# Running products of decays: the scan kept in program order, its second operand made by ScalarE in place, its rows in a buffer of their own

## The chip, the cores and the metric

The kernel runs on one core of one Trainium2 chip. The metric is device time in microseconds of that core. It has five engines with queues of their own: PE (TensorE, matmul), DVE (VectorE), ACT (ScalarE), POOL (GpSimd) and SP (SyncE, which here only issues DMAs). The kernel before takes 4147.79 us, the median of 3 runs (4133.58 to 4149.68).

## The reference, cut to what matters

A block takes x of 2 batches, 2048 tokens and 512 features and returns x + attention(xn) + experts(xn), with xn the layer norm of x. The attention is a gated delta rule over 16 heads of 128:

```python
q = silu(conv(x @ Wq)); k = silu(conv(x @ Wk)) * DK ** -0.5; v = silu(conv(x @ Wv))
alpha = sigmoid(x @ Wa + ba); beta = sigmoid(x @ Wb + bb)
def step(S, inps):                      # over 2048 tokens
    qt, kt, vt, at, bt = inps
    err = einsum('bhvk,bhk->bhv', S, kt) - vt
    S = at * S - bt * (err outer kt)
    return S, einsum('bhvk,bhk->bhv', S, qt)
```

and then a norm of each head, a gate and the product with Wo. The experts are 16, of which each of 512 tokens uses 4.

## The kernel before, in words

Tokens are taken in chunks of 128 (C), four chunks to a block of 512 (BLK), four blocks to a batch. Heads go in pairs (HG = 2). A pair of heads over one batch is a unit u; there are 16 units, 8 to a batch. Inside a chunk the token-by-token recurrence is replaced by matrix products, which need for each chunk a 128x128 matrix of decays: entry (j, i) is beta of token j times the product of alpha over the tokens j + 1 to i.

`keys(u)` (L163 to L221) makes what does not depend on the state. For each of four blocks and two heads it projects the keys (`proj`, L146), runs the convolution and silu (`conv_silu`, L124: on ACT a copy `raw` and a scaled copy `cv` out of PSUM, on DVE three taps, L137, on ACT the silu), and after a `yield` multiplies the keys with themselves (L201, bank `pk` of PSUM), makes the decay matrices of four chunks and multiplies both into `aT` (L214).

The four decay matrices come out of one running product. A row of 516 values (four times a zero and 128 alphas) is loaded to all 128 partitions (`row`, L180 to L184: a DMA from `a_d` of 258 KB into a tile `decA`, two buffers). POOL multiplies the matrix `unit` (a zero column and a unit matrix), repeated four times, with the betas of each chunk into `start` (L208, one buffer). DVE's `tensor_tensor_scan` (L212) computes state = row * state + start along the row, in place on the row: at each chunk the zero resets it, the diagonal puts beta in, and the alphas multiply on. The result is stored to `dec_d` (L213), read by `aT` (L214), and the next row is asked for (L218). `aT` is stored (L220).

`inverses(u)` (L223) inverts 32x32 blocks on POOL by some 60 small products in turn. `projection(n)` makes q, v and the gate of one block. `before`, `after` and `output` (L512, L580, L647) are the parts of a chunk step: matrix inverse from its blocks, state, output with its norm. In `after` the variance goes DVE (L641), POOL to the power of -1/2 (L642), and in `output` back to DVE (L656, `o`).

`recurrence(b, first)` (L668) walks the chunk steps of a batch in six ticks each and takes a step of every generator in turn; `keys(u + 2)` gets a step at ticks 0 and 3, so that its 16 steps fill the first 8 of a unit's 16 chunks. Units 0 and 1 have their keys made in the opening (`firsts`, L472), with the inverses of unit 0 between them. Batch 0 has the experts woven in (L894); `out_chunk` (L766) multiplies with Wo.

This nest is the program order. A planner then orders each engine's queue: it takes instructions by priority as soon as its own estimate has their operands ready, and so moves some ahead of their place in the program. Each engine runs its queue in the order written.

Of the kernel before, what the change touches and what calls it, by code (L numbers as in the profile page):

```python
# [7 lines left out]
F32 = mybir.dt.float32  # L8
I32 = mybir.dt.int32
AF = mybir.ActivationFunctionType  # L10
ALU = mybir.AluOpType
# [3 lines left out]
P = 128  # L15
NB, T, HID = 2, 2048, 512
H, D, KS = 16, 128, 4
C = 128
# [3 lines left out]
CB = BLK // C  # L22
NKT = HID // P
HG = 2
# [9 lines left out]
DW = C + 1  # L34
# [8 lines left out]
def block_kernel(ctx, tc, x, wq, wk, wv, wg, wo, wa, wb, ba, bb, par, consts,  # L43
                 topk_idx, topk_w, ew0, ew1, ew2, ewd0, ewd1, out):
    nc = tc.nc
# [7 lines left out]
    def bank(pool, tag):  # L53
        return pool.tile([P, 512], F32, tag=tag, name=tag)


    unit = cp.tile([P, DW], F32)
# [24 lines left out]
    for i in range(1, NQ, 2):  # L82
# [6 lines left out]
    bt = {}  # L89
# [8 lines left out]
            for p in range(3)]  # L98
# [4 lines left out]
    a_d = [dp.tile([H, NC * DW], F32, name=f"a_d{b}") for b in range(NB)]  # L103
    gin_d = [dp.tile([H, T], F32, name=f"gin_d{b}") for b in range(NB)]
    dec_d = [[[dp.tile([P, CB * HG * DW], F32, name=f"dec_d{b}_{p}_{k}") for k in range(NBK)]
              for p in range(NP)] for b in range(NB)]
# [13 lines left out]
    ap = ctx.enter_context(tc.tile_pool(name="first", bufs=1))  # L120
# [3 lines left out]
    def conv_silu(ps, p, h0, h, blk, dst):  # L124

        raw = cvp.tile([P, KS - 1 + BLK], F32, tag="raw", name="raw")
        if blk == 0:
            nc.gpsimd.memset(raw[:, 0:KS - 1], 0.0)
        else:
            nc.gpsimd.tensor_copy(raw[:, 0:KS - 1], halo[p][h])  # L130
        nc.scalar.copy(raw[:, KS - 1:], ps)  # L131
        if blk < NBK - 1:
            nc.gpsimd.tensor_copy(halo[p][h], raw[:, BLK:])  # L133
        cv = cvp.tile([P, BLK], F32, tag="cv", name="cv")
        nc.scalar.activation(cv, ps, AF.Identity, bias=cbias(p, h0 + h), scale=tap(p, h0 + h, KS - 1))  # L135
        for j in range(KS - 2, -1, -1):
            nc.vector.scalar_tensor_tensor(  # L137
                cv, raw[:, j:j + BLK], tap(p, h0 + h, j), cv, ALU.mult, ALU.add)
        nc.scalar.activation(dst, cv, AF.Silu)
# [6 lines left out]
    def proj(w, h, xt):  # L146
        ps = bank(ps_p, "p")
        for k in range(NKT):
            nc.tensor.matmul(ps, lhsT=w[:, k, h * D:(h + 1) * D], rhs=xt[k],  # L149
                             start=(k == 0), stop=(k == NKT - 1))  # L150
        return ps
# [4 lines left out]
    def beta_of():  # L156
        return ap.tile([P, NC, H], F32, tag="bt", name="bt")

    def load_wk(u):
        if u < NB * NP and u not in wks:  # L160
            wks[u] = load_w(ap, "wk", wk, u % NP * HG, f"wk{u}")

    def keys(u, xts, bank_k=(ps_p, "p")):  # L163

        b, hp = divmod(u, NP)
        h0 = hp * HG
        load_wk(u)
        w = wks[u]
        if u == NP:
            bt[b] = beta_of()
            nc.sync.dma_start(out=bt[b], in_=bt_d)
        n = CB * DW

        def row(blk, h):  # L180
            dec = ap.tile([P, n], F32, tag="decA", name="decA", bufs=2)
            nc.sync.dma_start(
                out=dec, in_=a_d[b][h0 + h, blk * n:(blk + 1) * n].partition_broadcast(P))
            return dec  # L184

        dec = row(0, 0)
        for blk in range(NBK):
            xt = xts(b, blk)
            for h in range(HG):
                ps = proj(w, h, xt)  # L190
                kt = ap.tile([P, BLK], F32, tag="kf", name="kf", bufs=2)
                conv_silu(ps, 1, h0, h, blk, kt)
                if (blk, h) == (NBK - 1, HG - 1):
                    if u + 1 != NP + 2:
                        load_wk(u + 1)
                nc.sync.dma_start(out=k_d[u][blk][h], in_=kt)
                yield
                pk = bank(*bank_k)
                for c in range(CB):
                    a = kt[:, c * C:(c + 1) * C]  # L200
                    nc.tensor.matmul(pk[:, c * C:(c + 1) * C], lhsT=a, rhs=a, start=True, stop=True)  # L201
                aT = ap.tile([P, CB, C], F32, tag="aTf", name="aTf", bufs=2)

                start = ap.tile([P, n], F32, tag="start", name="start")
                a = bt[b][:, blk * CB:(blk + 1) * CB, h0 + h:h0 + h + 1]
                nc.gpsimd.tensor_tensor(  # L208
                    start.rearrange("p (c j) -> p c j", c=CB),
                    bass.AP(unit.tensor, unit.offset, [unit.ap[0], (0, CB), unit.ap[1]]),  # L210
                    bass.AP(a.tensor, a.offset, [a.ap[0], a.ap[1], (0, DW)]), ALU.mult)
                nc.vector.tensor_tensor_scan(dec, dec, start, 0.0, ALU.mult, ALU.add)  # L212
                nc.sync.dma_start(out=dec_d[b][hp][blk][:, h * n:(h + 1) * n], in_=dec)  # L213
                nc.vector.scalar_tensor_tensor(  # L214
                    aT, pk.rearrange("p (c j) -> p c j", c=CB), -1.0 / D,
                    dec.rearrange("p (c j) -> p c j", c=CB)[:, :, 0:C], ALU.mult, ALU.mult)
                if (blk, h) != (NBK - 1, HG - 1):
                    dec = row(blk + (h + 1) // HG, (h + 1) % HG)  # L218
                o = h * NC + blk * CB
                nc.sync.dma_start(out=aT_d[u][:, o:o + CB, :], in_=aT)  # L220
                yield  # L221
# [124 lines left out]
    with ExitStack() as es:  # L346
# [125 lines left out]
        def firsts():  # L472
            for u in range(2):
                for _ in keys(u, get_xT, (ps_o, "o")):
                    yield
                if u == 0:
                    drain(inverses(0))
                    yield
# [189 lines left out]
    def recurrence(b, first):  # L668
# [21 lines left out]
        for m, at in enumerate([*steps, None, None]):  # L690
# [4 lines left out]
            if at:  # L695
                n, c = at
                u, blk = blocks[n]
                ci = blk * CB + c
                if c == 0:
                    for _ in nxt:  # L700
                        pass
                    nxt = projection(n + 1) if n + 1 < (b + 1) * NP * NBK else none
                    if blk == 0:
                        for _ in ks:
                            pass
                        if u + 2 < NB * NP:
                            ks = keys(u + 2, get_xT if (u + 2) // NP == b else ahead)
                        inv = inverses(u + 1) if u + 1 < NB * NP else None
                        if inv:
                            next(inv)  # L710
                if u == NB * NP - 1:

                    if ci == 1:
                        wos = load_wo(b)
                    if ci >= 4:
                        if c == 0:
                            slots.append(big())
                        for _ in last:
                            pass
                        last = out_chunk(b, ci - 4, wos, slots[ci % len(slots)])  # L720
# [290 lines left out]
```

## Time and profile before

| | us |
|---|---|
| median of 3 runs | 4147.79 (4133.58 to 4149.68) |
| profiled execution, its own time | 4144.64 |
| span of the profile, first to last instruction | 4142.8 |
| PE busy | 3870.6 |
| DVE busy | 2348.7 |
| POOL busy | 1909.0 |
| ACT busy | 1493.0 |
| mean granted PE clock | 0.981 of full |

The profile is one execution. A group's row gives line, engine, operation, output and inputs, shapes and count, then busy time and mean ns of one, then how long the engine stood idle just before these instructions and what released it. A busy PE is not PE at its peak, since the ends of matmuls are modelled.

### The profile page before, as it was taken

To read this page: it belongs to the slowest core of one execution; us is meant where nothing else is said; L and a number is where in the kernel's file an instruction comes from. 1 tells how busy PE (TensorE), PEld (TensorE's weight loads), DVE (VectorE), ACT (ScalarE), POOL (GpSimd) and SP (SyncE) were. 2 spreads that over 40 slices of the span, in tenths; PEclk is the share of its full clock that TensorE was granted. 3 is DMA by queue.
4 is the path that set the end of the run, shared out by engine and by line. 5 is a ranking of instruction groups with operands and counts; after the bars stand their busy time and mean duration, and the time that the engine had idled before them with its cause. 6 is when DMAs were issued, how large, how long until landed. Compare 5 with 4: busy or idle time off the path is not lost.

```text
span 4142.8 us, 58432 instructions
## 1 busy us (share of the span) xinstructions
PE 3870.6 (93%) x18046; PEld 2485.1 (60%) x18046; DVE 2348.7 (57%) x6132; ACT 1493.0 (36%) x3512; POOL 1909.0 (46%) x3624
## 2 busy tenths in 40 slices
PE   8789999999999999999989999999999999999999
PEld 6456666666666665656554456566656565666554
DVE  6655565565555557676651156666666666666221
ACT  3233333333333334444430034444444443444110
POOL 1556465474554645464550045454555555473100
PEclk9899999999999999999989999999999999999999
DMA  5455546455454544454564344343334334334322
GB/s 160 157 171 169 163 139 178 133 167 157 142 161 132 158 135 121 111 148 126 164 184 125 109 119 116 104 116 107 114 109 114 112 108 112 108 85 118 103 94 76
DMA packets 579701, 541.32 MB, mean 131 GB/s; under 512 B 354689, under 2 KB 421761, under 8 KB 574273
## 3 DMA queue, kind: packets, MB, share of 16 engines
q1 hardware_dynamic: 557280, 456.18, 37.9%
q0 software_dynamic: 22112, 81.41, 6.6%
q8 instruction: 147, 2.41, 0.2%
q14 instruction: 162, 1.32, 0.1%
HBM read 363.69 MB, written 173.67 MB: 130 GB/s over the span
## 4 chain that ended last, share of the span: by engine, by line
PE 40%; DVE 14%; DMA 8%; ACT 4%; POOL 4%; issue 3%; SPq 1%; POOLq 0%; DVEq 0%; ACTq 0%
PE p L149 16%; PE p L780 10%; DVE cv L137 8%; DMA decA<-a_d 5%; POOL qg L310 2%; PE c L605 2%; DVE decA L212 2%; PE c L614 2%; ACT cv L135 1%; PE l L535 1%; PE c L595 1%; PE p L931 1%; PE o L628 1%; PE o L631 1%; ACT raw L131 1%
## 5 line engine op out<-in xcount | busy, mean ns | idle before, releaser
L137 DVE SCALAR_TENSOR_TENSOR cv<-raw,prm,cv 128x512 f32<-128x512 f32 x1152 | 947.7, 823 | 261.8 <-ACT cv L135 245.9
L149 PE MATMUL p<-xT,wv 128*128 128x512 f32 x1024 | 488.4, 604 | 9.5 <-DVE xgT L921 5.7
L131 ACT COPY raw<-p 128x512 f32<-128x512 f32 x384 | 222.8, 580 | 745.5 <-PE p L149 722.2
L149 PE MATMUL p<-xT,wq 128*128 128x512 f32 x1024 | 482.1, 600 | 1.1 <-DVE act L934 0.6
L149 PE MATMUL p<-xT,wg 128*128 128x512 f32 x1024 | 476.6, 597 | 0.3
L780 PE MATMUL p<-wo,oTf 128*128 128x512 f32 x1024 | 454.8, 596 | 1.5 <-DMA oTf<-oT_d 1.5
L149 PE MATMUL p<-xT,wk 128*128 128x512 f32 x896 | 417.9, 604 | 1.9 <-ACT cv L135 1.2
L656 DVE TENSOR_SCALAR o<-o,mv,rs 128x128 f32<-128x128 f32 x512 | 187.1, 405 | 286.2 <-POOL rs L642 286.2
L780 PEld LDWEIGHTS p<-wo,oTf 128*128 128x128 f32 x1024 | 191.2, 192 | 220.0 <-issue 216.5
L564 POOL COPY inv<-iT 32x32 f32<-32x32 f32 x512 | 143.1, 279 | 357.4 <-DVE top L559 192.9
L208 POOL TENSOR_TENSOR start<-unit,bt 128x516 f32<-128x516 f32 x128 | 162.3, 1268 | 302.5 <-DVE decA L212 269.1
L135 ACT ACTIVATE cv<-p,prm 128x512 f32<-128x512 f32 x384 | 300.8, 783 | 0.2
L212 DVE TENSOR_TENSOR_SCAN decA<-decA,start 128x516 f32<-128x516 f32 x128 | 161.5, 1262 | 245.8 <-DMA decA<-a_d 168.2
L245 POOL TENSOR_TENSOR Y<-Y,t 128x30 f32<-128x30 f32 (+14 forms) x480 | 275.0, 573 | 36.9
L549 POOL TENSOR_TENSOR kg<-kv,gd 128x256 f32<-128x256 f32 x256 | 179.4, 701 | 235.1 <-ACT kv L547 229.4
L242 POOL TENSOR_TENSOR t<-Y 128x30 f32<-128x30 f32 (+14 forms) x480 | 269.7, 562 | 38.0 <-issue 0.2
L642 POOL TENSOR_TENSOR rs<-rs,mhalf 128x2 f32<-128x2 f32 x256 | 184.1, 719 | 206.0 <-DVE rs L641 198.1
L149 PEld LDWEIGHTS p<-xT,wv 128*128 128x128 f32 x1024 | 180.0, 194 | 154.4 <-issue 140.7
L149 PEld LDWEIGHTS p<-xT,wg 128*128 128x128 f32 x1024 | 180.6, 192 | 151.8 <-issue 151.1
L149 PEld LDWEIGHTS p<-xT,wq 128*128 128x128 f32 x1024 | 181.0, 193 | 150.2 <-issue 148.2
L133 POOL COPY halo<-raw 128x3 f32<-128x3 f32 x288 | 80.4, 279 | 400.1 <-ACT raw L131 392.9
L149 PEld LDWEIGHTS p<-xT,wk 128*128 128x128 f32 x896 | 162.9, 194 | 153.6 <-issue 151.0
(176 smaller groups left out, 7293.4 us busy)
## 6 DMA issues: line engine op xcount, KB each, us to landing
decA<-a_d SPq DMA_DIRECT2D x128, 258.0 KB
dec_d<-decA SPq DMA_DIRECT2D x128, 258.0 KB
decB<-dec_d SPq DMA_DIRECT2D x64, 516.0 KB
k_d<-kf SPq DMA_DIRECT2D x128, 256.0 KB
k<-k_d SPq DMA_DIRECT2D x64, 512.0 KB
aT_d<-aTf SPq DMA_DIRECT2D x128, 256.0 KB
gin<-gin_d SPq DMA_DIRECT2D x128, 256.0 KB
oT_d<-oT SPq DMA_DIRECT2D x256, 128.0 KB
```

The source lines that it names most:

```text
L131: nc.scalar.copy(raw[:, KS - 1:], ps)
L135: nc.scalar.activation(cv, ps, AF.Identity, bias=cbias(p, h0 + h), scale=tap(p, h0 + h, KS - 1))
L137: nc.vector.scalar_tensor_tensor(cv, raw[:, j:j + BLK], tap(p, h0 + h, j), cv, ALU.mult, ALU.add)
L149: nc.tensor.matmul(ps, lhsT=w[:, k, h * D:(h + 1) * D], rhs=xt[k], start=(k == 0), stop=(k == NKT - 1))
L208: nc.gpsimd.tensor_tensor(start.rearrange("p (c j) -> p c j", c=CB), bass.AP(unit.tensor, unit.offset, [unit.ap[0], (0, CB), unit.ap[1]]), ...
L212: nc.vector.tensor_tensor_scan(dec, dec, start, 0.0, ALU.mult, ALU.add)
L242: nc.gpsimd.tensor_tensor(t, bass.AP(col.tensor, col.offset, [col.ap[0], (Q, j), (0, n)]), bass.AP(row.tensor, row.offset, [row.ap[0], (0, ...
L245: nc.gpsimd.tensor_tensor(Y[:, 0:j, j + 1:], Y[:, 0:j, j + 1:], t, ALU.add)
L549: nc.gpsimd.tensor_tensor(kg, kv[:, 0], bcast(gd1[b][:, ci, hs], D), ALU.mult)
L642: nc.gpsimd.tensor_tensor(rs, rs, mhalf[:, 0:HG], ALU.pow)
L656: nc.vector.tensor_scalar(o[:, h, :], po[:, h * D:(h + 1) * D], mv[:, h, 0:1], rs[:, h:h + 1], ALU.subtract, ALU.mult)
L780: nc.tensor.matmul(py, lhsT=oT[:, h, :], rhs=wos[h], start=(h == 0), stop=(h == H - 1))
```

## The change

The row gets a tile `row` of its own (one buffer). The two `decA` buffers now hold the scan's second operand and its result: ACT fills each of the four chunks with `unit` scaled by the beta of each partition, and the scan works in place on that. POOL's product and its `start` tile are gone. The four activations and the scan are marked `keep_in_program_order`: such an instruction is issued behind the one that the program traced before it on its engine; what comes later in the program may still be moved ahead of it.

```diff
-        def row(blk, h):
-            dec = ap.tile([P, n], F32, tag="decA", name="decA", bufs=2)
+        def ask(blk, h):
+            row = ap.tile([P, n], F32, tag="row", name="row")
             nc.sync.dma_start(
-                out=dec, in_=a_d[b][h0 + h, blk * n:(blk + 1) * n].partition_broadcast(P))
-            return dec
+                out=row, in_=a_d[b][h0 + h, blk * n:(blk + 1) * n].partition_broadcast(P))
+            return row
...
-                start = ap.tile([P, n], F32, tag="start", name="start")
-                a = bt[b][:, blk * CB:(blk + 1) * CB, h0 + h:h0 + h + 1]
-                nc.gpsimd.tensor_tensor(
-                    start.rearrange("p (c j) -> p c j", c=CB),
-                    bass.AP(unit.tensor, unit.offset, [unit.ap[0], (0, CB), unit.ap[1]]),
-                    bass.AP(a.tensor, a.offset, [a.ap[0], a.ap[1], (0, DW)]), ALU.mult)
-                nc.vector.tensor_tensor_scan(dec, dec, start, 0.0, ALU.mult, ALU.add)
-                nc.sync.dma_start(out=dec_d[b][hp][blk][:, h * n:(h + 1) * n], in_=dec)
+                dec = ap.tile([P, CB, DW], F32, tag="decA", name="decA", bufs=2)
+                for c in range(CB):
+                    ci = blk * CB + c
+                    tc.keep_in_program_order(nc.scalar.activation(
+                        dec[:, c, :], unit, AF.Identity, scale=bt[b][:, ci, h0 + h:h0 + h + 1]))
+                flat = dec.rearrange("p c j -> p (c j)")
+                tc.keep_in_program_order(
+                    nc.vector.tensor_tensor_scan(flat, row, flat, 0.0, ALU.mult, ALU.add))
+                nc.sync.dma_start(out=dec_d[b][hp][blk][:, h * n:(h + 1) * n], in_=flat)
                 nc.vector.scalar_tensor_tensor(
-                    aT, pk.rearrange("p (c j) -> p c j", c=CB), -1.0 / D,
-                    dec.rearrange("p (c j) -> p c j", c=CB)[:, :, 0:C], ALU.mult, ALU.mult)
+                    aT, pk.rearrange("p (c j) -> p c j", c=CB), -1.0 / D, dec[:, :, 0:C],
+                    ALU.mult, ALU.mult)
                 if (blk, h) != (NBK - 1, HG - 1):
-                    dec = row(blk + (h + 1) // HG, (h + 1) % HG)
+                    row = ask(blk + (h + 1) // HG, (h + 1) % HG)
```

More of the change, by code (lines that the diff above doesn't have):

```diff
@@ L178, in keys @@
         n = CB * DW
-        def row(blk, h):
-            dec = ap.tile([P, n], F32, tag="decA", name="decA", bufs=2)
+        def ask(blk, h):
+            row = ap.tile([P, n], F32, tag="row", name="row")
             nc.sync.dma_start(
-                out=dec, in_=a_d[b][h0 + h, blk * n:(blk + 1) * n].partition_broadcast(P))
-            return dec
-        dec = row(0, 0)
+                out=row, in_=a_d[b][h0 + h, blk * n:(blk + 1) * n].partition_broadcast(P))
+            return row
+        row = ask(0, 0)
         for blk in range(NBK):
```

## The prediction

> **What bounds the kernel now.** I read the page first: busy times, the chain that ended last, the costliest groups.
>
> ```profile
> span 4142.8 us, 58432 instructions
> PE 3870.6 (93%) x18046; PEld 2485.1 (60%) x18046; DVE 2348.7 (57%) x6132; ACT 1493.0 (36%) x3512; POOL 1909.0 (46%) x3624
> PE 40%; DVE 14%; DMA 8%; ACT 4%; POOL 4%; issue 3%; SPq 1%; POOLq 0%; DVEq 0%; ACTq 0%
> PE p L149 16%; PE p L780 10%; DVE cv L137 8%; DMA decA<-a_d 5%; POOL qg L310 2%; PE c L605 2%; DVE decA L212 2%; PE c L614 2%; ACT cv L135 1%; PE l L535 1%; PE c L595 1%; PE p L931 1%; PE o L628 1%; PE o L631 1%; ACT raw L131 1%
> ...
> L656 DVE TENSOR_SCALAR o<-o,mv,rs 128x128 f32<-128x128 f32 x512 | 187.1, 405 | 286.2 <-POOL rs L642 286.2
> L208 POOL TENSOR_TENSOR start<-unit,bt 128x516 f32<-128x516 f32 x128 | 162.3, 1268 | 302.5 <-DVE decA L212 269.1
> L212 DVE TENSOR_TENSOR_SCAN decA<-decA,start 128x516 f32<-128x516 f32 x128 | 161.5, 1262 | 245.8 <-DMA decA<-a_d 168.2
> ```
>
> TensorE is busy 93% of the span and sets the end; but the chain passes for 5% of the span (207 us) through the load of the decay rows and for 2% through the scan on them. The scan's row says why: VectorE stands idle 245.8 us before its 128 scans. Next I asked for the scan's line: what it waits for, and who waits for it.
>
> ```profile
> its engine sat idle before it (us, times) until:
>   DMA decA<-a_d: 168.2, 78
>   issue: 32.4, 7
>   DMA a<-aT_d: 23.0, 6
> ...
> who waited for it (us, times):
>   POOL start L208: 269.1, 89
> ```
>
> Between 300 and 3600 us these waits are 239.5 us (158.1 before 2200, 81.4 after 2400); before 300 us they are 5.5. Then VectorE's timeline at one scan:
>
> ```profile
> 3231.14 2.33 DVE L137 SCALAR_TENSOR_TENSOR cv<-raw,prm,cv 128x512 f32<-128x512 f32 x3 [0.21 <-ACT cv L135]
> 3235.53 1.23 DVE L212 TENSOR_TENSOR_SCAN decA<-decA,start 128x516 f32<-128x516 f32 x1 [2.07 <-DMA decA<-a_d]
> 3236.68 3.35 DVE L137 SCALAR_TENSOR_TENSOR cv<-raw,prm,cv 128x512 f32<-128x512 f32 x3
> 3239.96 0.20 DVE L558 STREAM_TRANSPOSE iT<-l 128x32 f32<-128x32 f32 x1
> ```
>
> The row was asked for at 3231.06 and the scan could start 4.47 us later. The planner put the scan ahead of three conv taps and the transpose that the next inverse needs; all of them stand behind it. TensorE's next wait, 0.79 us at 3240.35, is for exactly that work (top, L559). So a late row becomes TensorE idle, in part. How much, the stretches by stage tell. The first half of each of fourteen units (8 chunks) carries eight scans, the second none:
>
> ```profile
> 491.00:638.00 147.00, 139.44 (x697) 92.69 (x695) 85.63 (x204) 53.52 (x126) 84.87 (x146) 0.99 0.51 153
> 752.00:900.00 148.00, 140.44 (x703) 94.75 (x702) 88.61 (x205) 53.69 (x126) 82.25 (x144) 0.98 0.48 144
> 1013.00:1167.00 154.00, 141.40 (x703) 93.67 (x702) 86.68 (x206) 53.94 (x127) 85.02 (x145) 0.98 0.49 145
> 1284.00:1436.00 152.00, 138.73 (x692) 92.28 (x691) 87.60 (x206) 54.13 (x128) 82.57 (x145) 0.99 0.48 146
> 2721.00:2806.00 85.00, 80.49 (x413) 53.94 (x414) 56.47 (x167) 39.99 (x100) 43.29 (x91) 1.00 0.41 115
> ```
>
> Columns: length, then busy us (instructions) of PE, PE loads, DVE, ACT, POOL, clock, DMA. The first four hold the same work. Idle before their scans was 23.0, 23.6, 34.0 and 31.6 us: 9.5 us more idle in the later pair goes with 5.5 us more length, a rate of 0.58. The last line has no scans and 4.5 us of PE idle in 85 (5.3%), the same share as scan halves of that time (2603 to 2721: 6.3 in 118). So there is structural idle too, which the change can't take.
>
> **The Trainium skill.** Perfetto Trace Analysis, Tensor Engine Instruction, says that VectorE, ScalarE and GpSimd are strict first-in first-out: one late operand holds all behind it. The timeline agrees. SBUF — State Buffer, Who interferes with whom, says that a VectorE instruction with two SBUF inputs contends with a GpSimd one that reads SBUF. Here the three taps beside a "start" product took 3.35 us in place of 3 x 0.751 (L137's median). ScalarE: Activation LUTs, What ACT_TABLE_LOAD costs, prices an ACTIVATE at 186 ns + 0.833 ns per element + 93 ns per pointer operand, with 93 ns overlap back to back; for cv (512 elements, two pointers) that gives 798 ns, and the trace has 783.
>
> **The change, part by part.** The order of TensorE's instructions hardly moves (some 250 of 9,900 stand elsewhere, many in the opening), so I cost the rest against this one.
>
> 1. Scan kept in program order: on VectorE it now stands behind L641 (rs) and ahead of o (L656), not ahead of taps. Its row is asked for right after the scan before, 14.9 us earlier in a scan half (119 us by 8), against the 4.3 to 4.5 us of the load. Removed: the 239.5 us of idle after 300 us.
> 2. Its new place is where VectorE waits for GpSimd's power (L642) anyway: in 2603 to 2721 that is 6.3 us over 8 waits, 0.79 each. Over 112 scans about 88 us of scan time falls into this wait. If GpSimd answers sooner now, less; bounds 0 to 138 (112 x 1.23).
> 3. GpSimd loses 128 x 1.268 = 162 us and the 269 us in which "start" stood at the head of its queue waiting for the scan, with inv, kg, rs and halo copies behind. VectorE also loses the contention: from 0 to (3.35 - 2.25) = 1.1 us a scan; I take 0.3, 34 us over 112.
> 4. ScalarE gains 512 activations of 128x129, one pointer. Estimate from the ScalarE page: 186 + 107 + 93 = 387 ns, four back to back 4 x 387 - 3 x 93 = 1.27 us. From this trace: copies of 512 and 256 columns (580, 381) give 281 ns for 128, and half of oT's excess over the 256 copy (563 - 381 = 182) makes 372 ns, 1.49 us without overlap. So 142 to 167 us after 300 us, and 20 to 24 before. They mostly stand behind the inv copies (L572) and ahead of or behind oT; next come q, inv (L576), raw and cv. ScalarE usually waits there: L576 and the others idle 0.3 to 2 us for PE or VectorE. I charge 5 us; without that cover it is the whole 1.27.
> 5. The row buffer is single (before, two decA buffers took the rows), and SP issues dec_d and then the next row. From scan to scan that is at least 1.23 + 0.32 + 0.4 + 4.3 = 6.3 us. In the opening the eight scans run from 86.2 to 120.75 us, 4.9 us apart; 7 x 1.3 = 9 us later, and unit 0's inverses wait behind them. Against it, GpSimd sheds some four "start" products with their waits between 125 and 200 us, where it is the busiest (18.6 of 20 us at 160 to 180): 6 to 10 us. I take 0, bounds -10 to +15.
> 6. aT and its bank of PSUM come some 1.6 us later behind the scan and one o; VectorE is ahead by the 2.07 us wait removed plus 1.23 of scan, so nothing. The DMAs are the same in number and size.
>
> **The sum.** Parts 1 to 3 free 239.5 + 88 + 34 = 361 us of VectorE. TensorE can't give all of that back: its visible idle in the fourteen halves is 2009 - 1890.9 = 118 us. At 0.58 part 1 alone would be 139 us, which exceeds it; at the unscanned share nothing would go. I take 55% of the idle: -65. With +5 (part 4) and 0 (part 5): -60. On the profiled execution's own 4144.6 us that is 4084.6; the median shown stands 3.2 higher (4147.8), so 4087.
>
> **The rivals.**
> - The pairs' rate holds in full: idle hidden behind modelled matmul ends comes back too. -139 less 5, some 4010. For it: the 207 us of chain. Against: the cap of 118 us.
> - Hidden anyway: VectorE only catches up later and PE's idle share stays at 5.3%, as in the halves without scans. Gain 0 to 20, about 4138.
> - Slower: ScalarE's blocks of four hold up oT, raw and cv, on which TensorE's PSUM banks wait. They price at 163 to 190 us; against -65 they decide from a pass-through of 0.37, and reach +0.5% at 0.5. At 0.6 of 175: +105 - 65, 4188. For it: strict order, and PE's two-deep banks. Against: ScalarE is 36% busy and waited 722 us for L149.
> - The change doesn't do what it says: GpSimd's power now comes late behind Y products, or the scan waits for its activations in place of the row. VectorE's wait would only change its name; the time is that of the second rival, and it shares its chance.
>
> **How the numbers follow.** Likeliest (-30 to -100): 0.50. Full rate: 0.22. Hidden: 0.16. Slower: 0.12. About 0.5%, 21 us, is what a measurement of this kernel can tell from no change. Faster 0.72, same 0.16, slower 0.12. The range from 4020 to 4148 leaves out the deepest part of the full rate and the slower case; the likeliest alone is 4048 to 4118.
>
> **What would show it.** Scan's idle for its row: near 0 (right), or replaced by ACT decA in step 4's place (wrong). Scan halves shorter by 3 to 5 us after 2400 and by 4 to 10 before 1500; halves without scans unchanged at 84 to 85. o's wait for rs down by some 80 us. ScalarE busy 1493 + 163 to 190. First eight scans 6.3 us apart. The prediction fails if oT, w or raw on ScalarE begin later relative to their matmuls and PE's waits for them grow.

## The result and the profile after

The changed kernel takes 4078.46 us (median of 4 runs, 4071.89 to 4085.75); the kernel before, run beside it, takes 4141.59 (4 runs, 4133.58 to 4149.68). The ratio is 0.9848, 95% interval 0.9817 to 0.9879: 63 us faster. The profiled execution took 4071.89 us, 72.8 less than that of before.

These are lines of the page of the changed kernel: span, busy times, the chain that ended last by engine and by line, and five groups. Lines of code behind L208 have moved down by one.

```profile
span 4070.1 us, 58930 instructions
PE 3825.9 (94%) x18046; PEld 2463.9 (61%) x18046; DVE 2337.3 (57%) x6132; ACT 1642.1 (40%) x4025; POOL 1822.5 (45%) x3496
PE 45%; DVE 12%; POOL 6%; ACT 5%; issue 2%; DMA 1%; SPq 0%; POOLq 0%; ACTq 0%; DVEq 0%
PE p L149 20%; PE p L781 11%; DVE cv L137 7%; POOL rs L643 2%; ACT cv L135 2%; PE c L615 2%; PE c L606 2%; POOL qg L311 2%; PE l L536 1%; PE o L629 1%; PE c L596 1%; PE o L632 1%; ACT raw L131 1%; PE p L932 1%; DVE o L657 1%
...
L149 PE MATMUL p<-xT,wk 128*128 128x512 f32 x896 | 417.2, 604 | 36.8 <-DVE aTf L215 29.7
L657 DVE TENSOR_SCALAR o<-o,mv,rs 128x128 f32<-128x128 f32 x512 | 194.8, 404 | 237.7 <-POOL rs L643 237.7
L643 POOL TENSOR_TENSOR rs<-rs,mhalf 128x2 f32<-128x2 f32 x256 | 229.0, 894 | 203.2 <-DVE rs L642 196.0
```

The row's load and the scan have left the chain: its DMA share is 1% where it was 8%. Two things are new. GpSimd's power (L643) is on it with 2%, at a mean of 894 ns where it had 719. And the key projections wait 29.7 us for `aT` (L215); before, they had 1.9 us of idle time in all. The scan's own line in the changed kernel shows what became of its wait:

```profile
L213 DVE TENSOR_TENSOR_SCAN decA<-row,decA x128: 1216/1225/2330, 86.7 to 3469.9; 128x516 f32<-128x516 f32 x128
...
its engine sat idle before it (us, times) until:
  DMA row<-a_d: 9.2, 9
who waited for it (us, times):
```

168.2 us of waiting for the row is 9.2, and nobody waits for the scan any more. The activations that make the operand (their line in the changed kernel) cost what the estimate said, a median of 390 ns against 387:

```profile
L209 ACT ACTIVATE decA<-unit,bt x512: 360/390/416, 77.1 to 3466.9; 128x129 f32<-128x129 f32 x171
```

The stretches of the changed kernel that answer to those of before, from the same chunk step to the same chunk step (columns as before: length; busy us and count of PE, PE loads, DVE, ACT, POOL; clock, DMA share, GB/s). The last has no scans:

```profile
506.00:650.00 144.00, 138.37 (x698) 91.76 (x697) 85.05 (x205) 62.00 (x154) 80.18 (x139) 1.00 0.52 159
760.00:905.00 145.00, 138.24 (x710) 92.52 (x709) 87.44 (x206) 62.66 (x156) 80.68 (x139) 1.00 0.51 154
1019.00:1165.00 146.00, 137.79 (x700) 91.68 (x699) 86.31 (x206) 62.09 (x154) 81.77 (x140) 1.00 0.51 153
1277.00:1420.00 143.00, 136.33 (x689) 90.49 (x690) 86.86 (x206) 60.97 (x152) 81.12 (x139) 1.00 0.51 159
2672.00:2757.00 85.00, 80.57 (x413) 54.03 (x414) 56.22 (x166) 40.91 (x103) 42.20 (x90) 1.00 0.38 106
```

The four with scans were 601 us long together and are 578; the one without is 85 as before. The two long ones of before, 154 and 152, have come close to the others. TensorE's idle time in the four fell from 41.0 us to 27.3. The other 9.3 us are taken out of what the profile calls busy PE (560.0 to 550.7), for nearly the same matmuls, and the clock column tells where they went: it was 0.98 or 0.99 and is 1.00. The trace's clock records have 20.4 us at half clock in the four stretches of before and none in those of the changed kernel. At half clock matmuls of 512 columns start 853 ns apart, at full clock 429 (medians), so half of such time is lost where TensorE has work: at most 10.2 us here.

So the time behind the opening has to be read in two parts, idle and granted clock. To see at which instruction TensorE lost time I took the starts of the matmuls: the distance from one start to the next, less the usual distance for that width (111 ns up to 128 columns, 429 ns for 512, in proportion between). What is over is called stall here. It needs no modelled end, and it has the slower pace at half clock in it.

| us, profiled executions | before | changed |
|---|---|---|
| stall, all matmuls | 479.2 | 406.5 |
| before r, inverse (L605, now L606) | 117.3 | 87.4 |
| before the inverse's own products (L567, L575, now L568, L576) | 123.3 | 47.6 |
| before the projections (L149) | 50.5 | 88.2 |
| first copy of `w`, where the recurrence begins | 276.1 | 289.9 |
| from there to the end | 3866.7 | 3780.2 |
| of that, TensorE idle in the profile | 217.0 | 169.1 |
| of that, time at half clock | 93.6 | 24.0 |

The inverses, which stood behind the waiting scan, give 75.7 us of stall back and `r` 29.9; the projections take 37.7. And the sum has two parts of opposite sign: the opening is 13.8 us longer, and all behind it is 86.5 us shorter. Of the 86.5, 47.9 are idle time of TensorE, and up to 34.8 (half of 69.6) go with the granted clock. The clock goes with the kernel, by and large: the changed kernel was granted 0.984 to 0.988 in its eight executions, here and in e5, and the kernel before 0.979 to 0.984 in all of those beside the experiments. From one execution to the next it still varies (24.0 us at half clock here, 37.5 in e5), and with half of that time taken off the two rests agree (3768.2 and 3767.0). Why the kernel before is granted less, no run shows.

### The profile page after: what moved, and what is told of

It is laid out like the page before. It is cut to its first block, busy times and chain, and to the rows that moved or that the text cites. A ratio compares the mean times of both kernels' runs of the same rounds, so it can differ in the third digit from the quotient of the medians.

```text
span 4070.1 us, 58930 instructions
## 1 busy us (share of the span) xinstructions
PE 3825.9 (94%) x18046; PEld 2463.9 (61%) x18046; DVE 2337.3 (57%) x6132; ACT 1642.1 (40%) x4025; POOL 1822.5 (45%) x3496
## 4 chain that ended last, share of the span: by engine, by line
PE 45%; DVE 12%; POOL 6%; ACT 5%; issue 2%; DMA 1%; SPq 0%; POOLq 0%; ACTq 0%; DVEq 0%
PE p L149 20%; PE p L781 11%; DVE cv L137 7%; POOL rs L643 2%; ACT cv L135 2%; PE c L615 2%; PE c L606 2%; POOL qg L311 2%; PE l L536 1%; PE o L629 1%; PE c L596 1%; PE o L632 1%; ACT raw L131 1%; PE p L932 1%; DVE o L657 1%
## 5 line engine op out<-in xcount | busy, mean ns | idle before, releaser
L137 DVE SCALAR_TENSOR_TENSOR cv<-raw,prm,cv 128x512 f32<-128x512 f32 x1152 | 921.8, 800 | 307.4 <-ACT cv L135 289.2
L149 PE MATMUL p<-xT,wv 128*128 128x512 f32 x1024 | 480.3, 596 | 4.6 <-DVE xgT L922 4.5
L149 PE MATMUL p<-xT,wq 128*128 128x512 f32 x1024 | 476.5, 595 | 7.4 <-DVE aTf L215 5.1
L149 PE MATMUL p<-xT,wg 128*128 128x512 f32 x1024 | 473.5, 594 | 3.9 <-ACT cv L135 3.5
L149 PE MATMUL p<-xT,wk 128*128 128x512 f32 x896 | 417.2, 604 | 36.8 <-DVE aTf L215 29.7
L643 POOL TENSOR_TENSOR rs<-rs,mhalf 128x2 f32<-128x2 f32 x256 | 229.0, 894 | 203.2 <-DVE rs L642 196.0
L133 POOL COPY halo<-raw 128x3 f32<-128x3 f32 x288 | 70.7, 245 | 528.3 <-ACT raw L131 523.5
L243 POOL TENSOR_TENSOR t<-Y 128x30 f32<-128x30 f32 (+14 forms) x480 | 278.0, 579 | 38.2 <-DMA dec_d<-decA 0.2
L149 PEld LDWEIGHTS p<-xT,wk 128*128 128x128 f32 x896 | 161.3, 192 | 193.8 <-issue 154.4
L559 DVE STREAM_TRANSPOSE iT<-l 128x32 f32<-128x32 f32 x256 | 55.4, 216 | 382.4 <-PE l L557 382.3
L149 PEld LDWEIGHTS p<-xT,wq 128*128 128x128 f32 x1024 | 179.2, 191 | 156.2 <-issue 147.6
L149 PEld LDWEIGHTS p<-xT,wg 128*128 128x128 f32 x1024 | 179.6, 191 | 155.5 <-issue 150.2
L149 PEld LDWEIGHTS p<-xT,wv 128*128 128x128 f32 x1024 | 178.2, 191 | 145.6 <-issue 139.7
L606 PEld LDWEIGHTS c<-r,inv 128*128 128x128 f32 x960 | 140.1, 191 | 148.3 <-issue 66.1
```

Source lines behind the costliest of these rows:

```text
L137: nc.vector.scalar_tensor_tensor(cv, raw[:, j:j + BLK], tap(p, h0 + h, j), cv, ALU.mult, ALU.add)
L243: nc.gpsimd.tensor_tensor(t, bass.AP(col.tensor, col.offset, [col.ap[0], (Q, j), (0, n)]), bass.AP(row.tensor, row.offset, [row.ap[0], (0, ...
L606: nc.tensor.matmul(pw[:, h * D:(h + 1) * D], lhsT=inv[:, h, :], rhs=r[:, h, :], start=True, stop=True)
L643: nc.gpsimd.tensor_tensor(rs, rs, mhalf[:, 0:HG], ALU.pow)
```

## The experiments

All ratios are to the kernel before on the same chip, with 95% intervals. Opening is the first copy of `w`, rest is from there to the end, and the last column is the time at half clock in the rest, of which at most half is lost; these three are from the one profiled execution. None of these kernels leaves out a part of the reference.

| run | time, us | ratio | opening | rest | at half clock |
|---|---|---|---|---|---|
| before (profile at the start) | | 1 | 276.1 | 3866.7 | 93.6 |
| changed | 4078.46 | 0.9848 [0.9817, 0.9879] | 289.9 | 3780.2 | 24.0 |
| e1 only the scan kept | 4079.63 | 0.9898 [0.9868, 0.9928] | 292.0 | 3786.6 | 35.6 |
| e2 no marks | 4019.44 | 0.9750 [0.9722, 0.9778] | 289.4 | 3730.6 | 31.6 |
| e3 two row buffers | 4068.14 | 0.9865 [0.9837, 0.9893] | 296.5 | 3776.6 | 37.9 |
| e4 activations twice | 4142.15 | 1.0046 [1.0029, 1.0063] | 284.3 | 3862.4 | 92.2 |
| e5 changed again | 4072.12 | 0.9857 [0.9833, 0.9880] | 289.5 | 3785.8 | 37.5 |
| e6 `pk` in another bank | 4042.25 | 0.9785 [0.9767, 0.9803] | 286.3 | 3755.5 | 85.3 |
| e7 no marks, two row buffers | 4015.38 | 0.9726 [0.9710, 0.9742] | 270.0 | 3730.3 | 34.1 |
| e8 GpSimd's operand, own row | 4056.36 | 0.9825 [0.9808, 0.9841] | 294.2 | 3756.6 | 30.7 |
| e9 kept, at an early place | 4023.06 | 0.9754 [0.9734, 0.9774] | 292.7 | 3718.7 | 20.5 |
| e10 no marks, activations twice | 4025.60 | 0.9754 [0.9735, 0.9774] | 285.9 | 3747.4 | 44.9 |
| e11 e9 with two row buffers | 4006.48 | 0.9690 [0.9673, 0.9707] | 271.3 | 3725.5 | 31.8 |

The kernel before had a median of 4121.18 us beside e1 to e4, 4130.62 beside e5 to e8, 4128.79 beside e9 and e10, and 4136.71 beside e11.

**e1: the order alone.** The kernel before, with only its scan marked:

```diff
-                nc.vector.tensor_tensor_scan(dec, dec, start, 0.0, ALU.mult, ALU.add)
+                tc.keep_in_program_order(
+                    nc.vector.tensor_tensor_scan(dec, dec, start, 0.0, ALU.mult, ALU.add))
```

> The kernel before with one edit: the scan alone is kept in program order. GpSimd still makes the second operand in a tile of its own, the scan still works in place on the row, in two buffers. Theory A (late rows behind a scan that was placed too early cost the time): the scan's idle for its row falls from 168 us to under 20, halves with scans shrink to 115 to 117 us, and the time is 50 to 65 us below before. Theory B (the gain is GpSimd's, which no longer carries 162 us of products nor waits 269 us at the head of its queue): within 15 us of before.

It is 42 us faster, less than expected, though the wait for the row is gone (1.9 us). `aT`'s line in e1 says what came in its place:

```profile
who waited for it (us, times):
  PEld p L149: 52.1, 43
  PE p L149: 43.8, 42
```

With the mark alone, and without ScalarE's operand, TensorE's projections wait for `aT`. So the new wait of the changed kernel comes from the scan's place, not from its activations.

**e2: the operand and the row alone.** The changed kernel without both marks.

```diff
-                    tc.keep_in_program_order(nc.scalar.activation(
-                        dec[:, c, :], unit, AF.Identity, scale=bt[b][:, ci, h0 + h:h0 + h + 1]))
+                    nc.scalar.activation(
+                        dec[:, c, :], unit, AF.Identity, scale=bt[b][:, ci, h0 + h:h0 + h + 1])
...
-                tc.keep_in_program_order(
-                    nc.vector.tensor_tensor_scan(flat, row, flat, 0.0, ALU.mult, ALU.add))
+                nc.vector.tensor_tensor_scan(flat, row, flat, 0.0, ALU.mult, ALU.add)
```

> The changed kernel without the two marks: ScalarE makes the operand in place, rows have a buffer of their own, but the planner places the scan and the activations where it likes. Theory A: the scan is early again and waits for its row, over 100 us of idle, and the time is within 20 us of before. Theory B: at least 40 us below before, whatever the scan waits for.

This was a surprise. It is 102 us faster than the kernel before, more than the whole change. The planner puts the scan early again, but the scan hardly waits; its line in e2:

```profile
L212 DVE TENSOR_TENSOR_SCAN decA<-row,decA x128: 1219/1296/1647, 85.3 to 3395.0; 128x516 f32<-128x516 f32 x128
its engine sat idle before it (us, times) until:
  DMA row<-a_d: 21.3, 9
  ACT decA L209: 15.7, 20
```

A row in a buffer of its own is free for the next load when the scan has read it. A row in `decA` was not: the scan worked in place on it, and the buffer stayed taken until the store and `aT` had read the result, and the row after next had to wait for that. The traces show it, by medians of the scans behind 300 us. In the kernel before, the next row is asked for 11.6 us behind the scan, 1.8 us behind the end of the `aT` of the scan before, whose buffer it takes. In e2 it is asked for 0.4 us behind the scan, some 11 us ahead of that `aT`. My theory had put the row's wait down to the order alone, and that part of it falls. No projection waits for `aT` in e2, and its rest is 49.6 us shorter than that of the changed kernel. From here on the question was what the marks cost.

**e3: a second row buffer.** The changed kernel with:

```diff
-            row = ap.tile([P, n], F32, tag="row", name="row")
+            row = ap.tile([P, n], F32, tag="row", name="row", bufs=2)
```

> The changed kernel with two row buffers in place of one. If the single buffer stretches the opening (first eight scans 6.8 us apart, before 4.9; first copy of w at 290 us, before 277), the spacing goes back towards 5, the first w comes 8 to 13 us earlier, and the time is 5 to 13 us below the changed kernel. If it is the marks that hold the opening's scans behind other work, or the activations, spacing and time stay (within 4 us).

The first eight scans run 5.1 us apart in place of 6.8, as expected, but the opening isn't shorter (296.5) and the time is that of the changed kernel.

**e4: ScalarE's work doubled.** Each activation is issued twice, with the same result:

```diff
-                for c in range(CB):
+                for c in list(range(CB)) * 2:
```

> The changed kernel with each of the 512 activations done twice, so ScalarE carries about 150 us more. If ScalarE's added work is hidden, as I charged it (5 us for the first 512), the time rises by 4 to 15 us. If ScalarE's blocks pass through to TensorE at a share of 0.4 or more, it rises by 60 us or more, and then the first 512 cost as much and the gain elsewhere is larger than 100 us.

The time goes up by 0.020 of that of before, 82 us in the rest, for 141 us more busy ScalarE (1642.1 to 1783.5). Up to 34 of the 82 go with the granted clock (92.2 us at half clock in place of 24.0), and TensorE's idle time in the rest is 49 us more. So ScalarE's work is not hidden at this place. `aT`'s line in e4 shows the way it takes:

```profile
who waited for it (us, times):
  PEld p L149: 87.2, 43
  PE p L149: 78.5, 43
```

The projections wait for `aT` as often as in the changed kernel (43 times) and some 1.8 times as long. The reading is that longer activations delay the scan, the scan delays `aT`, and `aT` delays the projections; e10 tests it.

**e5** is the changed kernel again, on the chip of the next three.

> The changed kernel itself, on the chip of these runs, to stand beside the others: 55 to 68 us below before, as the comparison on record (ratio 0.9848).

It comes out at the same ratio as in the first comparison, within the intervals.

**e6: another bank for `pk`.** The changed kernel, with the product of the keys in the banks of the chunk step's `l`, and not in the two banks of the projections:

```diff
-    def keys(u, xts, bank_k=(ps_p, "p")):
+    def keys(u, xts, bank_k=(ps_l, "l")):
```

> The changed kernel with the keys' products pk put into the three banks of PSUM that the chunk steps use, in place of the two of the projections. Theory C (the marks cost time since the scan runs just ahead of aT, aT is late, and the bank that pk holds keeps the next projection waiting): the waits of projections for aT vanish (91 us in the two rows of the changed kernel's waits) and the time falls by 25 to 45 us, unless the chunk steps now wait for banks instead, which their own waits would show. Rival D (the unmarked kernel is faster for its other order, not for the bank): no change beyond 10 us.

30 us faster than e5. No projection waits for `aT` now; `aT`'s line in e6:

```profile
who waited for it (us, times):
  PEld l L545: 48.9, 22
  PE l L545: 38.6, 21
```

The wait went with the bank: now the products at L545, which use the banks of `l`, have it, half as often. So it is a bank held too long. The rest is 24.7 us shorter than that of the changed kernel, and the granted clock hides part of what the bank is worth: e6 was at half clock for 85.3 us of it in place of 24.0 (its four executions were granted 0.980 to 0.983, those of e5 0.985 to 0.987). With half of that time, the most that it can have cost, taken off each, the rest is 55 us shorter.

**e7: e2 and the second row buffer together.**

> The kernel without marks (ScalarE's operand, rows of their own) with two row buffers. The single buffer's turn is 6.3 us; without marks the opening's scans stood 6.5 us apart (85.3 to 130.5). If the row was what spaced them, they come back to about 5 us and the time is 5 to 12 us below the unmarked kernel (4019 on an earlier chip, 0.975 of before): about 0.973. If not, the same within 5 us.

Without the marks the second buffer does shorten the opening, from 289.4 to 270.0, with scans 3.9 us apart; the rest is unchanged (3730.6 and 3730.3).

**e8: GpSimd's operand, the row in its own buffer.** The changed kernel without marks, and with the operand made by GpSimd as before, but in place in `decA`:

```diff
-                for c in range(CB):
-                    ci = blk * CB + c
-                    tc.keep_in_program_order(nc.scalar.activation(
-                        dec[:, c, :], unit, AF.Identity, scale=bt[b][:, ci, h0 + h:h0 + h + 1]))
+                a = bt[b][:, blk * CB:(blk + 1) * CB, h0 + h:h0 + h + 1]
+                nc.gpsimd.tensor_tensor(
+                    dec,
+                    bass.AP(unit.tensor, unit.offset, [unit.ap[0], (0, CB), unit.ap[1]]),
+                    bass.AP(a.tensor, a.offset, [a.ap[0], a.ap[1], (0, DW)]), ALU.mult)
```

> No marks, rows in a buffer of their own, but the operand made by GpSimd in place on decA, as one product of 128x516. Tells the row's buffer from the engine. If the early row is what frees the time: the scan's idle for its row is as low as without marks (about 20 us) and the time is 0.975 to 0.980 of before. If ScalarE's operand (GpSimd relieved by 162 us) gave it: no better than 0.99.

0.0175 faster than before against 0.0250 in e2: the buffer brings 70% of what e2 gains, and ScalarE's operand the other 0.0075 (31 us, give or take 13 by the two intervals). The scan's line in e8 shows one difference:

```profile
its engine sat idle before it (us, times) until:
  POOL decA L208: 137.0, 86
  DMA row<-a_d: 15.5, 6
```

The scan waits 137.0 us for GpSimd's product, where in e2 it waits 15.7 for ScalarE's. That this wait is what costs the 31 us isn't shown: in e9 and e10, below, the scan waits 72.9 and 64.2 us for its activations, and their times are those of e2. The other difference is GpSimd itself, which has its 128 products back.

**e9: both marks, at another place.** If the marks cost only through the place that they fix, then the same marks earlier in the program must cost nothing. The activations, the scan and the store are written ahead of the key projection, not behind the keys' product:

```diff
             for h in range(HG):
+                dec = ap.tile([P, CB, DW], F32, tag="decA", name="decA", bufs=2)
...
+                tc.keep_in_program_order(
+                    nc.vector.tensor_tensor_scan(flat, row, flat, 0.0, ALU.mult, ALU.add))
+                nc.sync.dma_start(out=dec_d[b][hp][blk][:, h * n:(h + 1) * n], in_=flat)
                 ps = proj(w, h, xt)
```

> The changed kernel with both marks, but the activations, the scan and its store traced three ticks earlier, ahead of the key projection, so that the marks pin them there and the scan is done well before aT. Theory C (the marks cost time only because they pin the scan just ahead of aT): the projections' waits for aT go from 90 us to under 20, and the time is 0.972 to 0.980 of before. Rival E (any pinning of ScalarE's and VectorE's queues costs, wherever it is): 0.983 or more.

It is as fast as e2, within the intervals. `aT`'s line in e9 has no projection at L149 among those who wait:

```profile
who waited for it (us, times):
  PE o L210: 12.8, 8
  PEld o L210: 10.7, 9
  PEld p L932: 1.3, 1
  PE p L932: 1.1, 1
```

The stall before L149 is 37.3 us, against 88.2 in the changed kernel. The marks cost nothing that these runs can tell; their place does.

**e10: activations doubled, without marks.** e2 with the edit of e4.

> The kernel without marks, with each of the 512 activations done twice. In the marked kernel doubling cost some 80 us, and the projections' waits for aT grew by 75. If ScalarE's added work reached TensorE by that route (activations, scan, aT, bank), then here, where the scan runs a step ahead of aT, doubling costs under 20 us against the unmarked kernel (0.975 of before): at most 0.980. If ScalarE delays TensorE's other inputs (w, bot, raw, cv) as well, it costs 40 us or more: 0.985 and up.

0.9754 against 0.9750 in e2: no difference in the time, within some 14 us by the two intervals. In the profiles the rest is 16.8 us longer and the opening 3.5 us shorter (the one of e10 is the slowest of its four executions). What costs 82 us in the rest at the late place costs 17 here. The scan's line in e10 shows that the wait is still there, but on VectorE, where it has room:

```profile
its engine sat idle before it (us, times) until:
  ACT decA L209: 64.2, 43
  DMA row<-a_d: 40.7, 19
```

**e11: e9 with two row buffers.**

> The kernel of the early marks with two row buffers. Two buffers moved the first copy of w from 289 to 270 us where nothing was marked, and not at all (290 to 296) where scan and activations were marked late. If it was the late place that took the opening's gain, the first w comes at 270 to 280 us here (293 with one buffer) and the time is 0.970 to 0.974 of before. If the marks as such hold the opening up, the first w stays at 290 or later and the time at 0.975.

The fastest of all, 0.9690: 3.1% below the kernel before, and clear of the changed one. The second buffer, which brought nothing in e3, shortens the opening from 292.7 to 271.3.

## Why the prediction was right, and where it was not

The time (4087 predicted, 4078.46 measured), the sign and the range hold. That the sum came so close is luck, since errors of both signs cancel: on the profiled execution -72.8 in place of -60, made of -86.5 behind the opening (predicted -60) and +13.8 in the opening (predicted 0), and the -86.5 has a part in it, the clock, that the prediction did not have.

**Part 1, the scan's wait.** Right as to what it removes: 168.2 us became 9.2, and the row was asked for a median of 14.2 us ahead of the scan (predicted 14.9). But the order was not needed for it: e2 has the scan early and only 21.3 us of that wait, since the row's own buffer lets it be asked for sooner. Either is enough: e1 has the order alone, and 1.9 us.

**Part 2, the scan under o's wait.** The mechanism is right and the size was off. The wait for `rs` fell by 48.5 us, not 88. VectorE's timeline in the changed kernel shows why:

```profile
2969.62 0.17 DVE L642 TENSOR_SCALAR rs<-mv 128x2 f32<-128x2 f32 x1
2969.70 1.23 DVE L213 TENSOR_TENSOR_SCAN decA<-row,decA 128x516 f32<-128x516 f32 x1
2971.45 0.41 DVE L657 TENSOR_SCALAR o<-o,mv,rs 128x128 f32<-128x128 f32 x1 [0.52 <-POOL rs L643]
2971.78 0.68 DVE L215 SCALAR_TENSOR_TENSOR aTf<-p,decA 128x512 f32<-128x512 f32 x1
```

and GpSimd's timeline in the same place:

```profile
2969.87 1.55 POOL L643 TENSOR_TENSOR rs<-rs,mhalf 128x2 f32<-128x2 f32 x1 [0.59 <-DVE rs L642]
```

The scan stands beside the very power that `o` waits for, and the power takes 1.55 us. In the whole trace 85 of the 256 powers overlap a scan, with a mean of 1246 ns; the other 171 have 719. That is 85 x 0.527 = 45 us, about what this term is off by (40). The prediction had named the page for this (the Trainium skill, SBUF — State Buffer, Who interferes with whom: a VectorE instruction with two SBUF inputs contends with a GpSimd one that reads SBUF) and used it only for what GpSimd's product cost VectorE, not for what the scan would cost GpSimd. The trace agrees with the page: in e2 and e9 no power overlaps a scan, and their means are 718 and 723 ns.

**Part 3, GpSimd's relief.** Right in kind: without it (e8 against e2) 31 us of the gain are missing. Whether they come through the scan's wait for GpSimd's product or through GpSimd's other work is open. The taps (L137) went from 823 ns to 800, 1152 x 0.023 = 26 us, where 34 was taken for less contention; but e8, which has GpSimd's products, stands at 811 and e2 at 805, so how much of it is contention isn't shown.

**Part 4, ScalarE.** The price was right: 390 ns against 387, a block of four 1.28 us (1.27 estimated), and 149 us more busy time where 163 to 190 was said. The reason for charging 5 us was not. "ScalarE usually waits there" doesn't make the block free when the scan and `aT` come right behind it: doubling it cost 82 us for some 124 us of work behind the opening (141 x 112/128), a pass-through of 0.66, or 0.39 with the 34 us of the clock taken off. That is the size of pass-through that the slower rival reckoned with (0.37 to 0.6), by a way that the prediction didn't name, through `aT` and not through oT, raw and cv. It didn't decide, since what the block replaced, GpSimd's product at the head of a queue, was no quicker: e1, with GpSimd's product and the scan at the same place, has a rest of 3786.6 against 3780.2, and with half of the time at half clock taken off they are equal (3768.8 and 3768.2).

**Part 5, the row buffer and the opening.** The scans came 6.8 us apart where at least 6.3 was predicted. Without the marks the mechanisms hold and the sizes don't: the single buffer costs 19.4 us (e2 to e7), not 9, and the relief is some 6 (before to e7, which has two row buffers as the kernel before had: 276.1 to 270.0), the low end of 6 to 10. The difference is close to the 13.8 measured, but the changed kernel need not have it from there: with a second row buffer it is no shorter in the opening (e3: 296.5), and e1, with two row buffers and the scan at the late place, is 15.9 longer too. So the late place is enough by itself, and the prediction had no term for that.

**Part 6 is the step that failed.** It said that `aT` and its bank come 1.6 us later, "VectorE is ahead by the 2.07 us wait removed plus 1.23 of scan, so nothing". From the end of the keys' product to the start of `aT` the median, for the scans behind 300 us, went from 1.53 us to 3.49. So it is 1.96 us later where 1.6 was said, and it is not for nothing. TensorE's timeline at the scan shown above:

```profile
2966.77 1.06 PE L201 MATMUL p<-kf 128*128 128x128 f32 x8
...
2972.52 0.70 PE L149 MATMUL p<-xT,wk 128*128 128x512 f32 x1 [0.36 <-DVE aTf L215]
```

The product was done at 2967.8 and its bank came free at 2972.5, behind a DVE queue of rs, scan, `o` held by the stretched power, and `aT`. There are two banks, and the next-but-one projection needs this one. VectorE being ahead is no help: the bank's time runs from TensorE's write, and TensorE had come forward as well. What it cost in the rest shows best when half of the time at half clock, the most that it can have cost, is taken off every run: against the changed kernel, e6, which changes the bank only, is 55 us shorter, and e2 and e9, which take the scan away from `aT`, are 53 and 60 shorter. As they stand the three are 25, 50 and 62 us shorter.

**The sum.** It took 65 us, 55% of TensorE's visible idle in the fourteen halves. Between the same chunk steps that idle was 119.6 us and is 79.4: 40 us came back, 34% of it. The halves with scans are 68.0 us shorter all the same, since they were at half clock for 51.0 us and are for 6.8, worth up to 22. The prediction had no term for the clock and gave no reason. The bank held longer kept more of it from coming back: e6, e2 and e9 bring it down to 45.9, 45.0 and 40.4 us, by 62 to 66%. So an idle term that was too large for this kernel stood in for a clock term that was missing. The cap itself held: no run gives back all 118 us. The rival that let the pairs' rate hold in full had the size of a kernel without the late place (e9 gives back 148.0 us in the rest, 139 was said), but not its ground: TensorE's visible idle in the rest fell by 104.2 us in e9, and the clock is worth up to 36.6, so little of it need have been hidden behind modelled ends.

**The signs that it named.** Between the same chunk steps, scan halves behind 2400 us are 113.1 to 113.5 us long where they were 118.1 to 120.8: 5.0 to 7.3 shorter, said were 3 to 5. Before 1500 us they are 3.3 to 7.9 shorter, said were 4 to 10. Halves without scans behind 2400 us are 84.5 to 84.9 where they were 83.9 to 85.0: unchanged, as said. So behind 2400 us, where the only time at half clock in these halves is 3.4 us in two of those of before, what is gained lies where the scans are. Before 1500 us that cannot be said: the halves without scans changed there too, by 5.4 us less to 1.2 us more, and about half of the time at half clock lay there.

**Still open.** Why two row buffers bring nothing in the opening as long as the kept scan stands late (e3: 296.5; e1, whose rows have two buffers too: 292.0), though the scans do come closer together. That the late place is the reason follows from e11 and e7; the chain inside the opening wasn't taken apart. Why e4, e6 and the kernel before are granted less clock than the others. By which way GpSimd's relief pays. Opening and rest are each from one execution of a kernel, and differences of a few us in them should not be read.

## What to carry to other kernels

When an instruction is moved, price it also by what then stands behind it on its queue: if the next one frees a PSUM bank, the time that the bank is held sets the next matmul, however far ahead that engine is on average. Ask first whether a late operand is late because of its buffer: here a buffer freed one step earlier did what the fixed order was thought to do, and without its price. And when TensorE's busy time changes though its matmuls don't, look at the granted clock before anything else; here up to 35 of 86.5 us went with it.

## What the hardware showed beyond that

- A GpSimd power on 128x2 values takes 712 ns by the median. Of the 85 in the changed kernel that overlap a scan of 128x516 on VectorE, 49 take over 1.4 us; all 49 begin while the scan is running. The 14 that begin ahead of it take 836 to 888 ns. The scan takes 1225 ns by the median in that kernel.
- The trace records TensorE's clock as full or half, never between: 29 stretches of half clock in the kernel before (157.1 us in all) and 11 in the changed one (97.7 us). A matmul of 512 columns follows the one before it after 853 ns there, and after 429 ns elsewhere. TensorE's busy time fell by 44.7 us with the same 18,046 matmuls; half of the 59.3 us less at half clock is 30 us of that, if TensorE had work in all of it.
